# An LSTM with a three-layer network behind it: when VectorE does its side work in the first 21 steps

## The chip, the cores and the metric

The kernel runs on one core of a Trainium2 chip. The metric is the device time of one execution in microseconds (us), and of several runs the median. Engines are named as in the profile: PE is TensorE (PEld its weight loads), DVE is VectorE, ACT is ScalarE, POOL is GpSimd, SP is SyncE.

## The reference

x has shape (32, 64, 256): 32 rows, 64 time steps, 256 features. An LSTM with 256 hidden units runs over the 64 steps, starting from the hidden state `cond_1024` and a cell state of zero. A network of three layers, whose weights are signs (+1 or -1, given as booleans), runs on every hidden state, and its result is added to x.

```python
xW = einsum('ntd,dg->ntg', x, Wx) + b
a = xw_t + prev_h @ Wh                      # one step; scan over 64 steps
i, f, o = sigmoid(a[:, :H]), sigmoid(a[:, H:2*H]), sigmoid(a[:, 2*H:3*H])
g = tanh(a[:, 3*H:])
next_c = f * prev_c + i * g
next_h = o * tanh(next_c)
...
h = concatenate([hs, -hs], axis=-1)         # 512 wide
h = relu(s0 * (h @ sign(k0))) * 2           # 512 -> 1024
h = relu(s1 * (h @ sign(k1))) * 2           # 1024 -> 1024
out = x + s2 * (h @ sign(k2))               # 1024 -> 256
```

## The kernel before

The 32 rows and 4 quarters of the hidden units share the 128 partitions, so a gate tile is 128 by 4 gates by 64. The recurrence takes 64 steps, one turn of the loop over `t` each. The order in which every engine gets its instructions is written out by hand in that loop: an engine does them in the order of the program text.

**One step of the recurrence.** `gates_from_h` (L277) lets PE add the product of h with wh to the gate banks. `cell_step` follows: ACT takes sigmoid, tanh and sigmoid (L294 to L296), DVE computes `kept`, `new` and `c` (L298 to L302), ACT takes tanh of c (L304), DVE computes `h` (L306) and turns it by a transpose into `hist` (L311), from which the next step's matmuls read. Meanwhile ACT copies the next step's share of x into the gate banks (`gates_from_x`, L288 and L289). The time from one step's first L277 matmul to the next step's is called a step's period here.

**The work beside it.** After the cell, each step issues a share of other matmuls. In the first 21 steps (`X_STEPS`) these are the products of x with wx (`x_products`, L230), 208 parts in all; each two time steps of x fill one bank in 8 parts, and a step issues 10 parts (8 in step 10). From step 21 on they are the network on blocks of 16 steps (`ffn_block`): layer 0 at L429, layer 1 at L456, layer 2 at L443. The last block runs after the loop, and its end is `last_chunk`.

**What DVE does for it in the first 21 steps.** When a bank of x products is full, `evict_x` adds the bias while it moves the bank to SBUF (`xg`, L245; 128x512). `next_x` turns the next half block of x by a transpose (`turn_x`, L217, into `xT`; 128x512) and then has SP load a half block further on (`load_x`). Every fourth step `split_h` writes h of four steps as two parts: `hhi` on ACT (L326) and `hlo` on DVE (L327; 128x256). `make_w0` builds a quarter of the layer-0 weights, first on ACT (`w0t`, L193) and then on DVE (L194; 128x512).

**What ACT does for it.** Besides L193 and L326, `make_w1` writes one of eight rows of the layer-1 weights (L199, 128x1024) and then has SP load further bits; `make_w2` writes a quarter of the layer-2 weights (L203, 128x512).

The pieces of weights wait in one queue, `chores`: four of w0, eight of w1, four of w2. One is taken in each step from `FIRST_CHORE` = 4 on. In the text of a step, the ACT part of the chore comes before the x products, the DVE part of a w0 chore after them, and the split of h at the very end of the steps 3, 7, 11 and so on:

```python
        later = chores.popleft()() if t >= FIRST_CHORE and chores else None
        ...
        if callable(later):
            later()
        if t % SH == SH - 1:
            split_h(t // SH)
```

Of the kernel before, what the change touches and what calls it, by code (L numbers as in the profile page):

```python
# [38 lines left out]
def lstm_ffn(ctx: ExitStack, tc: tile.TileContext, x, cond, wx_d, wh_d, b_d, k0_d, k1_d, k2_d, s0_d, s1_d, s2_d, out):  # L39
# [10 lines left out]
    SB = 16  # L50
    NB = T // SB
    TB = SB * N
    SH = 4
# [3 lines left out]
    AHEAD = 12  # L57
    X_STEPS = 21

    FIRST_CHORE = 4  # L60
    WARM_UP = 8

    const = ctx.enter_context(tc.tile_pool(name="const", bufs=1))
# [11 lines left out]
    def act(shape, dtype, name):  # L75
        return apool.tile(shape, dtype, tag="act", name=name)
# [4 lines left out]
    def load_x(i, half, engines, part=slice(0, SB // 2)):  # L81
        if part.start == 0:
            xq[i, half] = xpool.tile([P, SB // 2, HQ], F32, tag="x", name=f"x{i}_{half}")
        t0 = i * SB + half * (SB // 2)
        for q in range(NQ):
            engines[q % len(engines)].dma_start(
                out=xq[i, half][q * N : (q + 1) * N, part],
                in_=x[:, t0 + part.start : t0 + part.stop, ts(q, HQ)],
            )
# [57 lines left out]
    for i in range(2):  # L147
        t = act([P, 2, F0], U8, f"k0_{i}")
# [49 lines left out]
    def make_w1(k):  # L198
        nc.scalar.activation(w1[:, k, :], bits[k], AF.Identity, bias=nsgn[1], scale=sgn2[1])  # L199
        load_bits(4 + k)  # L200

    def make_w2(k, m):
        nc.scalar.activation(  # L203
            w2[:, m, ts(k, 4)].rearrange("p k (q j) -> p k q j", q=NQ),
            bits[FC0 + k].rearrange("p (k q m j) -> p m k q j", k=4, q=NQ, m=2)[:, m],
            AF.Identity,
            bias=minus1,
            scale=2.0,
        )
# [4 lines left out]
    def turn_x(i, half, part=slice(0, SB // 2)):  # L214
        if part.start == 0:
            xT[i, half] = act([P, SB // 2, 2, N], F32, f"xT{i}_{half}")
        nc.vector.transpose(  # L217
            xT[i, half][:, part].rearrange("p t b n -> p (t b n)"),
            xq[i, half][:, part].rearrange("p t j -> p (t j)"),
        )  # L220
# [2 lines left out]
    wh_q = wh.rearrange("p k (g q j) -> p k q g j", g=4, q=NQ)  # L223
    xg = {}

    def x_part(p, t, k, slots, start):

        i, s = divmod(t, SB // 2)
        for q in range(NQ):
            nc.tensor.matmul(  # L230
                p[q * N : (q + 1) * N, t % 2, slots],
                xT[i // 2, i % 2][:, s, k, :],
                wx_q[:, k, q, slots],
                start=start,
                stop=False,
                skip_group_check=True,
            )

    def x_bank(t):
        return ps_f.tile([P, 2, 4, HQ], F32, tag="pf", name=f"px{t}")  # L240

    def evict_x(p, t):
        xg[t] = gpool.tile([P, 2, 4 * HQ], F32, tag="xg", name=f"xg{t}")
        b = bias[:, :4].rearrange("p g j -> p (g j)").unsqueeze(1).to_broadcast([P, 2, 4 * HQ])
        nc.vector.tensor_tensor(xg[t], p.rearrange("p t g j -> p t (g j)"), b, ALU.add)  # L245

    def next_x(half):

        if half < 2 * NB:
            turn_x(*divmod(half, 2))  # L250
            if half + 4 < 2 * NB:
                load_x(*divmod(half + 4, 2), [nc.sync])

    def x_products(t0, t1):

        for t in range(t0, t1, 2):
            p = x_bank(t)
            for s in range(2):
                for k in range(2):
                    x_part(p, t + s, k, slice(0, 4), s == 0 and k == 0)  # L260
                    if s == 1 and k == 1:
                        evict_x(p, t)
                        half, left = divmod(t + 2, SB // 2)
                        if left == SB // 4 and t + 2 != AHEAD:
                            next_x(half + 1)
                    yield 2


# [4 lines left out]
    def gates_from_h(t, hT):  # L273
        for g, slots in zip(gates, (slice(0, 3), slice(3, 4))):
            for k in range(2):
                for q in range(NQ):
                    nc.tensor.matmul(  # L277
                        g[q * N : (q + 1) * N],
                        hT[:, k, :],
                        wh_q[:, k, q, slots],  # L280
                        start=False,
                        stop=(k == 1),
                        skip_group_check=True,
                    )
# [6 lines left out]
    def cell_step(t, c):  # L291
        sig = cell.tile([P, 3, HQ], F32, tag="sig", name=f"sig{t}")
        cand = cell.tile([P, HQ], F32, tag="cand", name=f"cand{t}")
        nc.scalar.activation(sig[:, 0:2, :], gates[0][:, 1:3], AF.Sigmoid)  # L294
        nc.scalar.activation(cand, gates[0][:, 0], AF.Tanh)  # L295
        nc.scalar.activation(sig[:, 2, :], gates[1][:, 0], AF.Sigmoid)  # L296
        kept = cell.tile([P, HQ], F32, tag="kept", name=f"kept{t}")
        nc.vector.tensor_mul(kept, sig[:, 1, :], c)  # L298
        new = cell.tile([P, HQ], F32, tag="new", name=f"new{t}")
        nc.vector.tensor_mul(new, sig[:, 0, :], cand)  # L300
        c = cell.tile([P, HQ], F32, tag="c", name=f"c{t}")
        nc.vector.tensor_add(c, kept, new)  # L302
        th = cell.tile([P, HQ], F32, tag="th", name=f"th{t}")
        nc.scalar.activation(th, c, AF.Tanh)  # L304
        h = cell.tile([P, HQ], F32, tag="h", name=f"h{t}")
        nc.vector.tensor_mul(h, sig[:, 2, :], th)  # L306
        i, s = divmod(t, SH)
        if s == 0:
            hist[i] = hpool.tile([P, 2, SH * N], F32, tag="hist", name=f"hist{i}")
        hT = hist[i][:, :, ts(s, N)]  # L310
        nc.vector.transpose(hT, h.rearrange("p (b j) -> p b j", b=2))  # L311
        if t + 1 < T:
            gates_from_x(t + 1)
        return c, hT

    def split_h(i):

        b, s = divmod(i, SB // SH)
        if s == 0:
            hparts[b] = (  # L320
                hpool.tile([P, 2, TB], F32R, tag="hhi", name=f"hhi{b}"),
                hpool.tile([P, 2, TB], F32R, tag="hlo", name=f"hlo{b}"),
            )
        hi, lo = (p[:, :, ts(s, SH * N)] for p in hparts[b])
        full = hist.pop(i)
        nc.scalar.copy(hi, full)  # L326
        nc.vector.tensor_tensor(lo, full, hi, ALU.subtract)  # L327
# [171 lines left out]
    for k, t in [(k, t) for t0 in (0, SB // 4) for k in range(2) for t in range(t0, t0 + SB // 4)]:  # L499
        x_part(banks[t // 2], t, k, early, t % 2 == 0 and k == 0)  # L500
    for t in range(SB // 2):
        for k in range(2):
            x_part(banks[t // 2], t, k, late, False)
        if t % 2:
            evict_x(banks[t // 2], t - 1)
        if t == 1:
            turn_x(0, 1)
    nc.vector.transpose(hT, h_first.rearrange("p (b j) -> p b j", b=2))
    for _ in x_products(SB // 2, AHEAD):
        pass  # L510
# [3 lines left out]
    def ffn():  # L514
        for b in range(NB):
            yield from ffn_block(b)


    chores = deque()
    chores += [lambda k=k, h=h: make_w0(k, h) for k in range(2) for h in range(2)]  # L520
    chores += [lambda k=k: make_w1(k) for k in range(FC0)]
    chores += [lambda k=k, m=m: make_w2(k, m) for k in range(2) for m in range(2)]

    work = x_products(AHEAD, T)
    total_x = (T - AHEAD) * 4
    total_ffn = (NB - 1) * (4 * FC0 + 2 * FC0 * FC1 + 4 * FC1)
    done = 0
    for t in range(T):
        gates_from_h(t, hT)
        c, hT = cell_step(t, c)  # L530
        if t == 0:
            next_x(AHEAD // (SB // 2) + 1)
        later = chores.popleft()() if t >= FIRST_CHORE and chores else None
        if outputs and next(outputs[0], "end") == "end":
            outputs.popleft()
        if t == X_STEPS:
            work, done = ffn(), 0
        goal = (t + 1) * total_x // X_STEPS if t < X_STEPS else (t + 1 - X_STEPS) * total_ffn // (T - X_STEPS)
        while done < goal:
            done += next(work)  # L540
        if t == X_STEPS - 1:
            next(work, None)
        if callable(later):
            later()
        if t % SH == SH - 1:
            split_h(t // SH)
    for n, _ in enumerate(work):
        if outputs and n % 4 == 0 and next(outputs[0], "end") == "end":
            outputs.popleft()
# [28 lines left out]
```

## Time and profile before

| what | value |
|---|---|
| median of 3 runs | 318.73 us (318.44, 318.73, 320.07) |
| the profiled execution, own time | 318.87 us |
| its span | 317.1 us |
| PE, PEld, DVE, ACT, POOL busy | 307.1, 237.5, 154.4, 130.1, 7.6 us |
| mean granted TensorE clock | 0.997 |
| first gates matmul of step 0 | at 19.84 us of the span |
| first gates matmul of step 21 | at 84.25 us of the span |

The median is the time to be predicted. The profiled execution is a run of its own: its time is the span that the trace covers and 1.77 us around it. "Busy" is time in which an engine had at least one instruction of its own in work. Matmuls overlap, so the busy time of PE says that it had work, not that it ran at its peak. In the timeline, a row gives the start, the length, the engine, the source line, the operation, what it writes and reads, and after an x the number of instructions that the row holds.

### The profile page before, as it was taken

The page shows a single profiled execution, that of the slowest core. Times are in us where ns is not written, and L with a number is a line of the kernel's source. Part 1 is how long each engine was busy: PE and PEld are TensorE (multiplying, and loading weights), DVE is VectorE, ACT ScalarE, POOL GpSimd, SP SyncE. Part 2 cuts the span into 40 slices and gives each one's busy share as a digit, 9 for nine tenths or more (in the row PEclk, how much of TensorE's full clock was granted, in tenths as well). Part 3 has the DMA queues.
Part 4 walks back from the last instruction along what each step waited for, and adds up shares of the span by engine and source line. Part 5 has one row for each costly group of instructions (what it writes and reads, how often), then busy time and mean ns, then how long its engine had stood idle before and what let it go on. Part 6 is the DMA issues. An engine that isn't in the chain of part 4 may idle for free.

```text
span 317.1 us, 9519 instructions
## 1 busy us (share of the span) xinstructions
PE 307.1 (97%) x4026; PEld 237.5 (75%) x4026; DVE 154.4 (49%) x475; ACT 130.1 (41%) x483; POOL 7.6 (2%) x26
## 2 busy tenths in 40 slices
PE   6789999999999999999999999999999999999994
PEld 3767777777877777777777777777777777888893
DVE  1355886756674443334845433466543433911124
ACT  0214557775563433334633434355333432511110
POOL 4400000000000000000000000000000000000000
PEclk9999999999999999999999999999999999999998
DMA  5755301142000000000010100000310000230002
GB/s 133 187 137 157 83 2 37 52 102 56 5 0 2 2 0 2 1 2 2 2 34 13 24 1 2 2 0 20 83 34 3 2 0 2 55 77 2 0 0 66
DMA packets 31001, 10.99 MB, mean 35 GB/s; under 512 B 28072, under 2 KB 30376, under 8 KB 30960
## 3 DMA queue, kind: packets, MB, share of 16 engines
q1 hardware_dynamic: 27648, 8.66, 11.4%
q10 hardware_dynamic: 3040, 1.57, 2.0%
q8 instruction: 31, 0.51, 0.7%
q0 software_dynamic: 272, 0.17, 0.2%
q14 instruction: 10, 0.08, 0.1%
HBM read 8.29 MB, written 2.10 MB: 33 GB/s over the span
## 4 chain that ended last, share of the span: by engine, by line
PE 89%; DMA 6%; DVE 3%; ACT 1%; issue 0%; ACTq 0%; SPq 0%; DVEq 0%
PE p L456 37%; PE gates L277 19%; PE px L230 12%; PE p L429 10%; PE po L443 7%; DMA x<-in_x_dram 2%; PE po L395 2%; DMA wx<-in_L_cond_Wx_dram 2%; PE p L383 1%; DMA wh<-in_L_cond_Wh_dram 1%; DVE xg L245 1%; DVE w L194 0%; ACT th L304 0%; DVE h L306 0%; DVE c L302 0%
## 5 line engine op out<-in xcount | busy, mean ns | idle before, releaser
L277 PEld LDWEIGHTS gates<-wh,hist 128*32 128x32 f32 x2016 | 54.3, 109 | 25.4 <-issue 14.1
L277 PE MATMUL gates<-wh,hist 128*32 128x192 f32 x2016 | 68.1, 275 | 0.4 <-DVE hist L311 0.3
L230 PE MATMUL px<-wx,xT 128*32 128x256 f32 (+1 forms) x1152 | 60.6, 356 | 2.8 <-DMA wx<-in_L_cond_Wx_dram 1.2
L294 ACT ACTIVATE sig<-gates 128x128 f32<-128x128 f32 x64 | 17.8, 278 | 81.5 <-PE gates L277 81.1
L230 PEld LDWEIGHTS px<-wx,xT 128*32 128x32 f32 x1152 | 39.8, 110 | 14.8 <-issue 2.2
L298 DVE TENSOR_TENSOR kept<-sig,c 128x64 f32<-128x64 f32 x63 | 14.1, 224 | 59.5 <-ACT sig L294 59.2
L304 ACT ACTIVATE th<-c 128x64 f32<-128x64 f32 x64 | 16.5, 257 | 31.2 <-DVE c L302 31.2
L429 PE MATMUL p<-hhi,w 128*128 128x512 f32 x64 | 25.5, 398 | 0.0
L429 PE MATMUL p<-hlo,w 128*128 128x512 f32 x64 | 25.3, 395 | 0.0
L306 DVE TENSOR_TENSOR h<-sig,th 128x64 f32<-128x64 f32 x64 | 14.5, 226 | 20.7 <-ACT th L304 20.7
L245 DVE TENSOR_TENSOR xg<-px,bias 128x512 f32<-128x512 f32 x32 | 20.9, 663 | 5.9 <-POOL nsgn L162 4.2
L288 ACT COPY gates<-xg 128x192 f32<-128x192 f32 x64 | 20.1, 313 | 0.0
L311 DVE STREAM_TRANSPOSE hist<-h 128x64 f32<-128x64 f32 x64 | 15.7, 246 | 2.4
L302 DVE TENSOR_TENSOR c<-kept,new 128x64 f32<-128x64 f32 x64 | 14.4, 225 | 2.2
L296 ACT ACTIVATE sig<-gates 128x64 f32<-128x64 f32 x64 | 15.0, 234 | 0.0
L429 PEld LDWEIGHTS p<-hhi,w 128*128 128x128 f32 x64 | 12.0, 188 | 2.8
L295 ACT ACTIVATE cand<-gates 128x64 f32<-128x64 f32 x64 | 14.0, 219 | 0.0
L300 DVE TENSOR_TENSOR new<-sig,cand 128x64 f32<-128x64 f32 x64 | 13.9, 218 | 0.0
L429 PEld LDWEIGHTS p<-hlo,w 128*128 128x128 f32 x64 | 12.0, 188 | 2.6
L289 ACT COPY gates<-xg 128x64 f32<-128x64 f32 x64 | 13.1, 204 | 0.0
L456 PE MATMUL p<-a_7h,w 128*128 128x512 f32 x31 | 12.6, 407 | 0.0
L456 PE MATMUL p<-a_2l,w 128*128 128x512 f32 x31 | 12.5, 404 | 0.0
(181 smaller groups left out, 516.7 us busy)
## 6 DMA issues: line engine op xcount, KB each, us to landing
x<-in_x_dram SPq DMA_DIRECT2D x58, 64.0 KB, 2.4
out_dram<-o SPq DMA_DIRECT2D x28, 64.0 KB, 1.8
bits<-in_L_ffn_k_dram SPq DMA_DIRECT2D x10, 128.0 KB, 2.8
wx<-in_L_cond_Wx_dram SPq DMA_DIRECT2D x8, 64.0 KB, 3.2
wx<-in_L_cond_Wx_dram ACTq DMA_DIRECT2D x8, 64.0 KB, 3.2
k<-in_L_ffn_k_dram SPq DMA_DIRECT2D x8, 64.0 KB, 2.6
wh<-in_L_cond_Wh_dram SPq DMA_DIRECT2D x2, 192.0 KB, 4.5
wh<-in_L_cond_Wh_dram ACTq DMA_DIRECT2D x2, 192.0 KB, 5.2
```

The lines of the kernel that those rows point to most:

```text
L230: nc.tensor.matmul(p[q * N : (q + 1) * N, t % 2, slots], xT[i // 2, i % 2][:, s, k, :], wx_q[:, k, q, slots], start=start, stop=False, ski ...
L245: nc.vector.tensor_tensor(xg[t], p.rearrange("p t g j -> p t (g j)"), b, ALU.add)
L277: nc.tensor.matmul(g[q * N : (q + 1) * N], hT[:, k, :], wh_q[:, k, q, slots], start=False, stop=(k == 1), skip_group_check=True,)
L288: nc.scalar.copy(gates[0], x_t[:, :3])
L294: nc.scalar.activation(sig[:, 0:2, :], gates[0][:, 1:3], AF.Sigmoid)
L296: nc.scalar.activation(sig[:, 2, :], gates[1][:, 0], AF.Sigmoid)
L304: nc.scalar.activation(th, c, AF.Tanh)
L306: nc.vector.tensor_mul(h, sig[:, 2, :], th)
L311: nc.vector.transpose(hT, h.rearrange("p (b j) -> p b j", b=2))
L429: nc.tensor.matmul(p, w0[:, k, ts(m, P)], a[:, k, :], start=(n == 0), stop=(n == 3))
L443: nc.tensor.matmul(po[m], w2[:, m, k], a1[k][n], start=(k == 0 and n == 0), stop=(k == FC1 - 1 and n == 1))
L456: nc.tensor.matmul(p1[m], w1[:, k, ts(m, P)], a0[k][n], start=(k == 0 and n == 0), stop=(k == FC0 - 1 and n == 1),)
```

## The change

The loop gets a count, `load`, of the bias additions and turns of x that a step has put on DVE. Turns of x are no longer done where they fall due: `x_products` puts them into a queue, `turns`, earlier than before (after the second time step of a half block instead of the fourth), and one is taken at the end of a step that has fewer than two such operations. If one is still waiting after the sixth time step, it is done there. The turn that step 0 did right after the cell now goes this way too, behind the step's bias addition.

The split of h goes into a queue, `splits`. It is taken at the end of a step with a count below two, and at the latest four steps after it fell due; from step 21 on it is taken at once, as before. A step that takes a split takes no chore. The chores start in step 2 instead of 4. The DVE part of a w0 chore goes into a queue as well, `w0_parts`, and is taken at the end of a step with a count below two, or in step 20. The four w2 chores have a queue of their own and start in step 24.

The resulting order, with the DVE work behind the cell in each of the first steps:

| step | before | after |
|---|---|---|
| 0 | turn, addition | addition, turn |
| 1 | addition | addition |
| 2 | addition | addition, turn |
| 3 | addition, turn, addition, split | two additions |
| 4 | addition, w0 | addition, split |
| 5 | addition, w0 | addition, turn |
| 6 | addition, turn, w0 | addition, w0 |
| 7 | two additions, w0, split | two additions |
| 8 | addition | addition, turn |
| 9 | addition, turn | addition, split |
| 10 | addition | addition, w0 |
| 11 | addition, split | addition, split |
| 12 | two additions, turn | two additions |
| 13 | addition | addition, turn |
| 14 | addition | addition, w0 |
| 15 | addition, split | addition, turn |
| 16 | addition, turn, addition | two additions |
| 17 | addition | addition, split |
| 18 | addition | addition, w0 |
| 19 | addition, split | addition, split |
| 20 | two additions | two additions |

On ACT, the w0 pieces move from steps 4 to 7 to steps 2, 3, 5 and 6; the w1 pieces from steps 8 to 15 to steps 7, 8, 10 and 12 to 16; the w2 pieces from steps 16 to 19 to steps 24, 25, 26 and 28. The order of PE's matmuls and of SP's loads is the same in both kernels, and so is the number of instructions on each engine.

```diff
-    FIRST_CHORE = 4
+    FIRST_CHORE = 2
+    W2_STEP = 24
...
+    load = [0]
+    turns = deque()
+
...
     def evict_x(p, t):
...
+        load[0] += 1
         nc.vector.tensor_tensor(xg[t], p.rearrange("p t g j -> p t (g j)"), b, ALU.add)
 
     def next_x(half):
 
         if half < 2 * NB:
+            load[0] += 1
             turn_x(*divmod(half, 2))
...
                         half, left = divmod(t + 2, SB // 2)
-                        if left == SB // 4 and t + 2 != AHEAD:
-                            next_x(half + 1)
+                        if left == 2 and half + 1 < 2 * NB:
+                            turns.append(half + 1)
+                        if left == 6 and turns:
+                            next_x(turns.popleft())
...
-    chores += [lambda k=k, m=m: make_w2(k, m) for k in range(2) for m in range(2)]
+    chores2 = deque(lambda k=k, m=m: make_w2(k, m) for k in range(2) for m in range(2))
+    splits, w0_parts = deque(), deque()
...
     for t in range(T):
+        load[0] = 0
         gates_from_h(t, hT)
         c, hT = cell_step(t, c)
-        if t == 0:
-            next_x(AHEAD // (SB // 2) + 1)
-        later = chores.popleft()() if t >= FIRST_CHORE and chores else None
+        if t % SH == SH - 1:
+            splits.append(t // SH)
...
-        if callable(later):
-            later()
-        if t % SH == SH - 1:
-            split_h(t // SH)
+
+        if turns and load[0] < 2:
+            next_x(turns.popleft())
+        if splits and (load[0] < 2 or t >= X_STEPS or t == SH * splits[0] + 2 * SH - 1):
+            split_h(splits.popleft())
+        else:
+            if t >= FIRST_CHORE and chores:
+                part = chores.popleft()()
+                if part is not None:
+                    w0_parts.append(part)
+            elif t >= W2_STEP and chores2:
+                chores2.popleft()()
+            if w0_parts and (load[0] < 2 or t == X_STEPS - 1):
+                w0_parts.popleft()()
```

## The prediction, written before the changed kernel ran

> **What bounds the kernel now.** I read the page's busy line first. PE is busy for 97% of the span, DVE for 49%:
>
> ```profile
> PE 307.1 (97%) x4026; PEld 237.5 (75%) x4026; DVE 154.4 (49%) x475; ACT 130.1 (41%) x483; POOL 7.6 (2%) x26
> ```
>
> So a change to DVE's work can pay only where DVE makes PE late. The table of stages shows where to look: from 100 to 260 us PE is busy in every microsecond, so the network steps have no hole that this change could fill. The holes lie before 20 us, where loads are awaited and which the change leaves alone, and in the stage of the x products, 20 to 85 us. There I went through PE's timeline, whose rows alternate between the gates matmuls (L277) and a step's x products (L230). These are steps 3, 4 and 5, then 8 to 11, then 18 and 19:
>
> ```profile
> 28.93 1.08 PE L277 MATMUL gates<-wh,hist 128*32 128x192 f32 x32
> 31.96 1.08 PE L277 MATMUL gates<-wh,hist 128*32 128x192 f32 x32
> 35.26 1.08 PE L277 MATMUL gates<-wh,hist 128*32 128x192 f32 x32
> ...
> 44.35 1.08 PE L277 MATMUL gates<-wh,hist 128*32 128x192 f32 x32
> 47.87 1.08 PE L277 MATMUL gates<-wh,hist 128*32 128x192 f32 x32 [0.27 <-DVE hist L311]
> 50.90 1.08 PE L277 MATMUL gates<-wh,hist 128*32 128x192 f32 x32
> 51.77 1.94 PE L230 MATMUL px<-wx,xT 128*32 128x256 f32 x32
> 53.78 1.08 PE L277 MATMUL gates<-wh,hist 128*32 128x192 f32 x32
> ...
> 75.03 1.08 PE L277 MATMUL gates<-wh,hist 128*32 128x192 f32 x32
> 78.19 1.08 PE L277 MATMUL gates<-wh,hist 128*32 128x192 f32 x32
> ```
>
> The usual period is 3.03 us (28.93 to 31.96): 72 matmuls that PE issues without a gap. Step 10 has 32 x products instead of 40 and a period of 2.88 us (50.90 to 53.78); there PE waits, and 2.88 us is what the chain gates, sigmoid, cell, `hist`, gates itself takes. The chain thus has 3.03 - 2.88 = 0.15 us to spare in a usual step. Steps 4 and 8 take 3.30 and 3.52 us, 0.27 and 0.49 too long. Step 13 takes 3.06, step 17 3.04, step 18 3.16. From step 0 to step 21 the trace has 84.25 - 19.84 = 64.41 us; twenty periods of 3.03 and one of 2.88 make 63.48. All that can be won in this stage is 0.93 us.
>
> The full timeline shows why step 4 is long:
>
> ```profile
> 31.59 0.65 DVE L245 TENSOR_TENSOR xg<-px,bias 128x512 f32<-128x512 f32 x1
> 32.16 0.69 DVE L217 STREAM_TRANSPOSE xT<-x 128x512 f32<-128x512 f32 x1
> 32.78 0.65 DVE L245 TENSOR_TENSOR xg<-px,bias 128x512 f32<-128x512 f32 x1
> 32.94 0.28 ACT L294 ACTIVATE sig<-gates 128x128 f32<-128x128 f32 x1 [0.84 <-PE gates L277]
> 33.35 0.40 DVE L327 TENSOR_TENSOR hlo<-hist,hhi 128x256 fp32r<-128x256 f32 x1
> 33.68 0.21 DVE L298 TENSOR_TENSOR kept<-sig,c 128x64 f32<-128x64 f32 x1
> ```
>
> An undisturbed `kept` starts 0.31 us after its `sig` (29.91 to 30.22), so here 33.25 would have been in time. It started at 33.68, 0.43 late, because step 3 had queued four operations ahead of it. With 0.15 to spare that makes 0.28, and PE shows 0.27. Step 8 checks this: `sig` at 45.33, `kept` at 46.29, 0.65 late, less 0.15 is 0.50; PE shows 0.49. In steps 7, 13 and 17 `kept` is 0.16, 0.21 and 0.18 late (42.77, 61.34 and 73.46, against `sig` at 42.30, 60.82 and 72.97), which costs 0.00, 0.03 and 0.01. So the rule that I use is: period = 3.03 + (lateness of `kept` - 0.15), where that is positive.
>
> **The change part by part.** *Fewer operations behind the cell.* The tails of steps 3, 7, 12 and 16 (which made steps 4, 8, 13 and 17 late) become two additions each. DVE's room runs from the end of `hist` (28.64) to the next `kept` (30.22), 1.58 us. Two additions took 1.25 us in step 7 (44.13), 1.33 in step 20 (83.87), where the second starts after its bank is full. They fit, so the four long periods fall to 3.03: 0.27 + 0.49 + 0.03 + 0.01 = 0.80 us saved.
>
> *What is late next.* The fullest new tails are addition and turn (steps 0, 2, 5, 8, 13, 15) and addition and w0 part (6, 10, 14, 18). Both exist before: addition and turn in step 9 ended at 51.79 with `kept` at 52.19; addition and w0 part in step 4 ended at 36.43 with `kept` at 36.55, on time. In steps 0, 8 and 13 the bank is full only with the fourth of five parts; such an addition (step 17, 74.86) took 0.69 instead of 0.65 and was done 0.67 after `hist`, so with 0.69 of turn the tail ends 1.36 after it, inside 1.58. Step 0 may start 0.15 later, since its turn no longer fills the wait for the bank; that still ends at about 1.51. I charge nothing; the cover is 0.07 to 0.3 us of room and 0.15 of spare chain, and beyond it each further 0.1 us costs 0.1 in each of six steps. PE then finds nothing else late: 3.03 us is its own issue.
>
> *Turned x for PE.* A turn is needed when the next half block's first x product issues. The tightest is step 13 (before: step 12): its products come after the third part of step 14, about 1.1 us after the turn ends. The others lie whole steps ahead. Cost nothing. The four loads that SP issues behind each turn move with it, by at most 3 us of a queue that then has nothing else due; the bits behind the w1 pieces are loaded a step earlier for the first and at most one later for the last.
>
> *Chores on ACT.* ACT's room is the same stretch. A w0 piece (0.72 us) in steps 2 and 3 meets room of 1.45 us (the idle time before `sig` at 29.91). A w1 piece of 1.24 us fits: in step 9 it ended at 51.61 with `sig` at 51.88. Before, steps 11 and 15 held a w1 piece and the split, 1.24 + 0.39; after, a split has its step for itself. The first w0 piece now stands at about 28.45 at the head of ACT's queue, and everything of ACT waits behind it if k0 has not landed; SP issued k0's last load at 24.2 and the slowest took 3.3, so it is there by 27.5. Cost nothing; the next use is far: the last w0 part in step 18 against layer 0 at 85.26, the last w1 piece in step 16 against layer 1 at 95.1.
>
> *w2 in the network steps.* Four pieces of 0.72 us join ACT in steps 24, 25, 26 and 28. Steps there take 4.18 or 4.41 us against a chain of 2.88. The worst is step 26: the eviction `a_2h` starts at 109.89 and ends at 110.49, the piece runs to about 111.21, and `sig`, which came at 110.77, waits 0.44 us. `hist` then ends at 113.02 instead of 112.58, still 0.94 before the gates matmuls at 113.96. Layer 2 first reads w2 at 110.79, the pieces of steps 24 and 25 by then done. Cost nothing; without that cover, 0.44 for this piece and at most 4 x 0.72 = 2.88 for all.
>
> *Unknown.* Step 18's extra 0.13 has another face: `sig` started 1.25 us after the gates matmuls instead of 0.98, with ACT idle. No row says why. Since instructions move, it may vanish (-0.13) or strike elsewhere; bounded by its 0.27 of lateness, it is -0.13 to +0.27 and I take zero.
>
> The sum: 318.87 - 0.80 = 318.07 for the profiled execution. The median stands 0.14 below that execution, so 318.73 - 0.80 = 317.93, a change of -0.25%. About 0.5%, 1.6 us, is what a measurement of this kernel can tell from no change.
>
> **Rivals.** *Nothing moves.* The view of waits puts only 0.3 us of PE's idle time on `hist`, in one step, and four of the six addition-and-turn tails come where there was less before. If the new tails each give back a little, the gain is 0 to 0.3 us: 318.4 to 318.7. Against it: the rule above reproduces all five late periods within 0.02 us. The Trainium skill ("Perfetto Trace Analysis", Identifying the Most-Contended Engine) says to find the engine with the highest occupancy and optimize that first; by it, work on DVE at 49% beside PE at 97% would leave 318.73. The trace disagrees in part: in two steps of 64 DVE's queue does set PE's start.
>
> *The w2 pieces hold up the network steps (slower).* If ACT's queue in steps 24 to 28 decided PE's start, each piece would cost up to its 0.72: 318.73 - 0.80 + 2.88 = 320.8. It decides once the lateness of `sig` passes 0.94 us in step 26, against my 0.44; two pieces in one step would be needed. For it speaks only that these are the one place where the change adds work.
>
> *A smaller loss of the same kind:* 0 to 1.6 us lost to new waits (late k0, late banks, a stray late `sig`), 318.7 to 320.3.
>
> *More than 0.93 us gained* would need a second mechanism, of which the trace shows none.
>
> **How the numbers follow.** Forecast, -0.65 to -0.93 us: 0.68. Nothing moves: 0.15. The small loss: 0.08. The w2 pieces, or another loss above 1.6 us: 0.06. A gain above 1.6 us: 0.03. Within 0.5% lie the first three, 0.91. The range begins at 318.73 - 0.93 - 0.29 = 317.5 (everything won, and the 0.29 by which the fastest run shown lies below the median) and ends at 318.73 + 0.44 = 319.1 (nothing won, and step 26's piece uncovered). It holds the first two cases and a third of the small loss.
>
> **What would show it.** Right: periods of 3.03 in steps 4 and 8, no `kept` more than 0.15 behind its time in steps 0 to 20, step 21 starting at about 83.45 instead of 84.25, and from there to the end the same length as before. Wrong: a period above 3.05 in steps 1, 3, 6, 9, 14 or 16 (behind addition and turn); an ACT idle time before the first w0 piece put on k0; PE idle between 97 and 115 us; or the stage shortened and the time unchanged.

## The result and the profile after

The changed kernel takes 317.63 us in the median of 22 runs, the kernel before 318.40 in 22. The ratio is 0.9967, with a 95% interval of 0.9955 to 0.9979: 0.33% faster, and this interval leaves no room for "no change". (0.9967 is also the ratio of the means; the medians differ by 0.77 us, 0.24%.) The forecast was 317.93. The profiled execution took 318.01 us with a span of 316.2 (before 318.87 and 317.1).

From the page of the changed kernel come the busy line and the line with the engines' shares of the chain that ended last:

```profile
PE 306.8 (97%) x4026; PEld 238.4 (75%) x4026; DVE 155.5 (49%) x475; ACT 130.2 (41%) x483; POOL 7.6 (2%) x26
PE 91%; DMA 6%; DVE 1%; ACT 0%; issue 0%; SPq 0%; ACTq 0%
```

The busy shares are those of before to the percent. What changed is the second line. In the profile of before it reads:

```profile
PE 89%; DMA 6%; DVE 3%; ACT 1%; issue 0%; ACTq 0%; SPq 0%; DVEq 0%
```

DVE's share fell from 3% to 1%, and PE's rose from 89% to 91%. DVE works as much as it did, but no longer in the way.

PE's timeline after, the gates matmuls of steps 3 to 5, 8 to 10, and 18 and 19:

```profile
28.98 1.08 PE L285 MATMUL gates<-wh,hist 128*32 128x192 f32 x32
32.01 1.08 PE L285 MATMUL gates<-wh,hist 128*32 128x192 f32 x32
35.04 1.08 PE L285 MATMUL gates<-wh,hist 128*32 128x192 f32 x32
...
44.14 1.08 PE L285 MATMUL gates<-wh,hist 128*32 128x192 f32 x32
47.17 1.08 PE L285 MATMUL gates<-wh,hist 128*32 128x192 f32 x32
50.20 1.08 PE L285 MATMUL gates<-wh,hist 128*32 128x192 f32 x32
...
74.30 1.08 PE L285 MATMUL gates<-wh,hist 128*32 128x192 f32 x32
77.33 1.08 PE L285 MATMUL gates<-wh,hist 128*32 128x192 f32 x32
```

Steps 4 and 8 now take 3.03 us each (32.01 to 35.04, 44.14 to 47.17), where they took 3.30 and 3.52; step 18 takes 3.03 instead of 3.16; and the remark that PE waits for `hist` is gone. From the full timeline of the tail behind step 7, which held four operations before, these are DVE's rows and the first sigmoid:

```profile
43.59 0.24 DVE L319 STREAM_TRANSPOSE hist<-h 128x64 f32<-128x64 f32 x1
43.76 1.33 DVE L250 TENSOR_TENSOR xg<-px,bias 128x512 f32<-128x512 f32 x2
45.11 0.28 ACT L302 ACTIVATE sig<-gates 128x128 f32<-128x128 f32 x1 [0.28 <-PE gates L285]
45.42 0.23 DVE L306 TENSOR_TENSOR kept<-sig,c 128x64 f32<-128x64 f32 x1 [0.33 <-ACT sig L302]
```

The two additions end at 45.09, before `sig` has even started, and `kept` follows 0.31 us behind `sig`, on time.

To compare kernels I take the time from the first sigmoid of step 0 to that of step 21 (the stage of the x products), and from there to that of step 63. Beside them stand the start of the first sigmoid and the timed result as a ratio to before with its interval:

| kernel | step 0 starts, us | step 0 to 21 | 21 to 63 | ratio |
|---|---|---|---|---|
| before | 20.82 | 64.40 | 179.20 | 1 |
| changed | 20.86 | 63.51 | 179.21 | 0.9967 (0.9955 to 0.9979) |
| `again` | 20.25 | 63.51 | 179.20 | 0.9986 (0.9969 to 1.0003) |
| `turns_only` | 21.61 | 64.06 | 179.21 | 1.0008 (0.9989 to 1.0026) |
| `parts_only` | 21.15 | 63.53 | 179.20 | 0.9978 (0.9958 to 0.9999) |
| `w2_late` | 20.76 | 64.27 | 179.22 | 0.9996 (0.9976 to 1.0016) |
| `extra1` | 21.43 | 64.76 | 179.20 | 0.9999 (0.9980 to 1.0018) |
| `extra2` | 20.96 | 78.49 | 179.20 | 1.0430 (1.0404 to 1.0455) |
| `one_more` | 20.99 | 64.28 | 179.20 | 0.9976 (0.9959 to 0.9993) |
| `two_more` | 21.66 | 63.67 | 179.20 | 0.9977 (0.9963 to 0.9990) |

The stage is 64.40 - 63.51 = 0.89 us shorter, and nothing behind it moved. The start of step 0 scatters over 1.4 us between these executions, more than the effect, so the timed ratios, of 4 to 12 runs each below the row of the changed kernel, can't tell the middle rows apart; the stage can, to a few hundredths. The 0.89 us is 0.28% of the time, inside the interval of the timed ratio. An interval that excludes 1 is not enough by itself: that of `one_more` does so too, though its stage is only 0.12 us, or 0.04% of the time, shorter. What ties the gain to the change is the stage, not the timed ratio alone.

### The profile page after: what moved, and what is told of

Its sections match the earlier page's. It is cut to its first block, busy times and chain, and to the rows that moved or that the text cites. A ratio compares the mean times of both kernels' runs of the same rounds, so it can differ in the third digit from the quotient of the medians.

```text
span 316.2 us, 9515 instructions
## 1 busy us (share of the span) xinstructions
PE 306.8 (97%) x4026; PEld 238.4 (75%) x4026; DVE 155.5 (49%) x475; ACT 130.2 (41%) x483; POOL 7.6 (2%) x26
## 4 chain that ended last, share of the span: by engine, by line
PE 91%; DMA 6%; DVE 1%; ACT 0%; issue 0%; SPq 0%; ACTq 0%
PE p L464 37%; PE gates L285 20%; PE px L234 14%; PE p L437 10%; PE po L451 7%; DMA x<-in_x_dram 3%; PE po L403 2%; DMA wx<-in_L_cond_Wx_dram 2%; PE p L391 1%; DMA wh<-in_L_cond_Wh_dram 1%; DVE a_7l L345 0%; SPq L87 0%; DVE o L370 0%; DVE o L367 0%; ACT sig L302 0%
## 5 line engine op out<-in xcount | busy, mean ns | idle before, releaser
L285 PEld LDWEIGHTS gates<-wh,hist 128*32 128x32 f32 x2016 | 55.1, 109 | 23.6 <-issue 13.4
```

What stands on the lines that cost most here:

```text
L285: nc.tensor.matmul(g[q * N : (q + 1) * N], hT[:, k, :], wh_q[:, k, q, slots], start=False, stop=(k == 1), skip_group_check=True,)
```

## The experiments

**The changed kernel again.**

> The changed kernel once more. Theory (VectorE's queue behind the cell made four gate starts late, and nothing else changed): every period from step 0 to step 20 is 3.03 us (2.87 in step 10), the first gates matmul of step 21 comes 63.5 us after that of step 0 (64.4 before), and the time is about 0.8 us below before. Rival (the medians of the two kernels differ by more than that because of how the execution starts or ends): the difference between executions of this kernel lies ahead of the first gates matmul (19.89 us in its first trace) or behind the last one, at the same 63.5 us between.

The stage is 63.51 us again. The span fell from 316.2 to 315.6, and all of it lies ahead of step 0, whose matmuls started 0.62 us earlier; the shorter wait of PE for a load of x is 0.40 of it. PE's timeline of `again`:

```profile
19.27 1.08 PE L285 MATMUL gates<-wh,hT_first 128*32 128x192 f32 x32 [0.59 <-DMA x<-in_x_dram]
```

In the changed kernel's first trace this row stood at 19.89 with a wait of 0.99. So the theory holds for the stage, and the rival for the difference between these two executions, which lies ahead of step 0. The 0.89 us is not part of that. The time itself was a miss: about 0.8 us below before was expected, and these 12 runs have a median 0.45 us below (318.49 against 318.94), with an interval of 0.9969 to 1.0003 that does not exclude "no change".

**One part of the change at a time.** `turns_only` is the kernel before with this change alone (the count of operations goes with it):

```diff
-                        if left == SB // 4 and t + 2 != AHEAD:
-                            next_x(half + 1)
+                        if left == 2 and half + 1 < 2 * NB:
+                            turns.append(half + 1)
+                        if left == 6 and turns:
+                            next_x(turns.popleft())
...
-        if t == 0:
-            next_x(AHEAD // (SB // 2) + 1)
...
+        if turns and load[0] < 2:
+            next_x(turns.popleft())
         if callable(later):
             later()
```

> The kernel before with the turns of x queued as in the change, and the splits and weight pieces as they were. Theory, with the rule period = 3.03 + (lateness of kept - 0.15) and the tails of this order (two additions, w0 part and split in step 7 are left): kept is about 0.54 late in step 8 and 0.17 in step 6, so 64.3 - 0.4 = 63.9 us from step 0 to step 21, half of the gain. Rival (the turns make the gain, by way of loads and turned x that come earlier): 63.5.

`parts_only` is the changed kernel with the first lines put back:

```diff
-                        if left == 2 and half + 1 < 2 * NB:
-                            turns.append(half + 1)
-                        if left == 6 and turns:
-                            next_x(turns.popleft())
+                        if left == SB // 4 and t + 2 != AHEAD:
+                            next_x(half + 1)
...
         c, hT = cell_step(t, c)
+        if t == 0:
+            next_x(AHEAD // (SB // 2) + 1)
```

> The changed kernel with the turns of x where they were; splits, w0 parts and w2 pieces wait as in the change. Theory: steps 3, 12 and 16 still hold two additions and a turn, which makes kept 0.12 to 0.18 late in steps 4, 13 and 17, so nearly inside the 0.15 to spare: 63.5 to 63.6 us from step 0 to step 21, almost the whole gain. Rival (the turns make the gain): 64.3.

`turns_only` has 64.06 us: step 4 is cured, step 8 is not. From its timeline behind step 7, DVE's rows and the first sigmoid:

```profile
44.50 1.33 DVE L249 TENSOR_TENSOR xg<-px,bias 128x512 f32<-128x512 f32 x2
45.75 0.74 DVE L194 SCALAR_TENSOR_TENSOR w<-k,nsgn,w0t 128x512 fp32r<-128x512 uint8 x1
45.85 0.28 ACT L301 ACTIVATE sig<-gates 128x128 f32<-128x128 f32 x1 [0.50 <-PE gates L284]
46.41 0.42 DVE L334 TENSOR_TENSOR hlo<-hist,hhi 128x256 fp32r<-128x256 f32 x1
46.74 0.22 DVE L305 TENSOR_TENSOR kept<-sig,c 128x64 f32<-128x64 f32 x1
```

`kept` should have come at 45.85 + 0.31 = 46.16 and came at 46.74, 0.58 late (0.54 expected); the rule charges 0.58 - 0.15 = 0.43, and the period is 3.46. Most of what lies above the expected 63.9 is a late sigmoid in step 18 (0.12), treated below. `parts_only` has 63.53: behind step 3 it still queues addition, turn and addition.

```profile
33.27 0.28 ACT L300 ACTIVATE sig<-gates 128x128 f32<-128x128 f32 x1 [0.80 <-PE gates L283]
33.69 0.20 DVE L304 TENSOR_TENSOR kept<-sig,c 128x64 f32<-128x64 f32 x1
```

`kept` is 0.42 behind `sig`, 0.11 late, and the period stays 3.03, as the 0.15 to spare says; only step 13, 0.22 late, shows 3.06. The two parts overlap, since either one cures step 4. Letting the splits and w0 parts wait was nearly the whole cure, and on top of it the earlier turns added 0.02.

**More work in the tails.** `extra1` and `extra2` add one and two more operations to VectorE's tail:

```diff
+    spare = const.tile([P, 2, 4 * HQ], F32, name="spare")
+
+    def extra(t):
+        b = bias[:, :4].rearrange("p g j -> p (g j)").unsqueeze(1).to_broadcast([P, 2, 4 * HQ])
+        nc.vector.tensor_tensor(spare, xg[t // 2 * 2], b, ALU.add)
...
+        if t < X_STEPS - 1:
+            for _ in range(1):        # 2 in extra2
+                extra(t)
```

> The changed kernel with one more bias addition of 128x512 (into a tile that nobody reads) at the end of VectorE's tail in each of the steps 0 to 19. Theory, by the rule with the tails of this order: kept comes 0.1 to 0.35 us late in most steps, of which 0.15 is spare, so 64.7 us from step 0 to step 21 instead of 63.5, 1.2 us lost for 12 us of added work. Rival (VectorE at 49% is not what bounds the stage): 63.5, no loss.

> The same with two more additions in each of the steps 0 to 19. Theory: now every step is the length of chain and tail together, kept is 0.6 to 0.9 late in nearly all, and the stage takes 75.7 us: the second 12 us of work cost 11. Rival (a busy share matters, not the place): 63.5 to 64.7 and no kink between one and two additions.

64.76 us was measured against 64.7 expected: 20 added operations, some 12 us of VectorE's work, cost 1.25. The second 20 operations cost 13.7, since now nearly every step is as long as its chain and tail. 78.49 is 2.8 above the expected 75.7. DVE's rows in one tail of `extra2` point to what was mis-sized:

```profile
45.12 0.65 DVE L250 TENSOR_TENSOR xg<-px,bias 128x512 f32<-128x512 f32 x1
45.70 0.73 DVE L195 SCALAR_TENSOR_TENSOR w<-k,nsgn,w0t 128x512 fp32r<-128x512 uint8 x1
46.35 1.41 DVE L256 TENSOR_TENSOR spare<-xg,bias 128x512 f32<-128x512 f32 x2
47.67 0.22 DVE L312 TENSOR_TENSOR kept<-sig,c 128x64 f32<-128x64 f32 x1
```

The two added ones occupy 47.67 - 46.35 = 1.32, or 0.66 each. The expectation does not give what it put for one; 2.8 us over 40 operations is 0.07, which brings it to about 0.59, near the 0.60 from start to start of two additions from a bank (1.25 - 0.65). That this was the mis-sized term is worked back, not shown. The rule itself holds in these long steps: the `sig` of this step starts at 46.32, so `kept` is 47.67 - 46.32 - 0.31 = 1.04 late, the rule gives 3.03 + 0.89 = 3.92, and the period is 3.91. The kink between one and two is there, and busy share is not what prices VectorE's work here.

**The w2 pieces alone.** The kernel before with the four w2 pieces in the steps where the change has them:

```diff
-    chores += [lambda k=k, m=m: make_w2(k, m) for k in range(2) for m in range(2)]
+    chores2 = [lambda k=k, m=m: make_w2(k, m) for k in range(2) for m in range(2)]
+    chores2 = dict(zip((24, 25, 26, 28), chores2))
...
+        if t in chores2:
+            chores2[t]()
```

> The kernel before with only the four w2 pieces moved from steps 16 to 19 to steps 24, 25, 26 and 28. Theory: VectorE's order is that of before, so 64.3 us from step 0 to step 21 (64.4 if step 18's late sigmoid comes again) and the time of before within 0.1 us. Rival (taking work off ScalarE in the x steps makes part of the gain): less than 64.2, periods 4 and 8 shorter than 3.30 and 3.52. Second rival (the pieces cost time in the network steps): a gap of PE between steps 25 and 29 and up to 2.9 us more.

Periods 4 and 8 are 3.29 and 3.51, so taking work off ScalarE cures neither. The network steps take 179.22 us: the pieces cost nothing there. But the stage is 64.27, 0.13 shorter than before. All of it is in step 18, whose sigmoid is on time.

**The late sigmoid of step 18.** ScalarE's timeline of before and of the changed kernel:

```profile
76.28 0.28 ACT L294 ACTIVATE sig<-gates 128x128 f32<-128x128 f32 x1 [0.92 <-PE gates L277]
76.46 0.22 ACT L295 ACTIVATE cand<-gates 128x64 f32<-128x64 f32 x1
76.56 0.23 ACT L296 ACTIVATE sig<-gates 128x64 f32<-128x64 f32 x1
```

```profile
75.27 0.28 ACT L302 ACTIVATE sig<-gates 128x128 f32<-128x128 f32 x1 [1.12 <-PE gates L285]
75.45 0.22 ACT L303 ACTIVATE cand<-gates 128x64 f32<-128x64 f32 x1
75.78 0.22 ACT L304 ACTIVATE sig<-gates 128x64 f32<-128x64 f32 x1
```

Before, the first of the three starts 1.25 us after the gates matmuls (75.03) instead of 0.98. After, the first two are on time and the third comes 0.51 us behind the first instead of 0.28. The delay has not gone, it has moved by two instructions, to where `h` does not need the result yet. Counted along ScalarE's instruction list, the late one is number 149 in both: the changed kernel has two instructions fewer ahead of step 18. Two kernels test this by the number alone:

```diff
     nc.scalar.activation(warm[:, 1:2], warm[:, :1], AF.Sigmoid)
+    nc.scalar.activation(warm[:, 2:3], warm[:, :1], AF.Sigmoid)      # one_more: before with this line
+    nc.scalar.activation(warm[:, 3:4], warm[:, :1], AF.Sigmoid)      # two_more: changed kernel with both
```

> The kernel before with one more instruction at the head of ScalarE's list (the tiny warm-up sigmoid a second time). Theory (the sigmoid that came 0.27 us late in step 18 did so because of its place in ScalarE's instruction list: in six traces it is always the instruction that stands at number 149 which starts 0.23 to 0.27 us late): the first sigmoid of step 18 is now number 150 and on time, number 149 is the w2 piece of step 17, period 17 of the sigmoids is 3.04 instead of 3.31, and 64.27 us from step 0 to step 21 instead of 64.40. Rival (it has to do with the w2 pieces, which stood beside it in both kernels that showed it): period 17 stays at 3.31.

> The changed kernel with two more of the tiny warm-up sigmoids at the head of ScalarE's list, so that number 149 of the list, which was the third activation of step 18, is its first one. Theory (the number decides): the first sigmoid of step 18 comes 0.27 us late again, period 17 of the sigmoids is 3.30 instead of 3.03, and the stage takes 63.63 us instead of 63.51, though VectorE's order is the changed one. Rival (the changed order itself removed it): 63.5 and no period above 3.05.

`one_more` did as expected: the sigmoid of step 18 is on time, period 17 is 3.03, the stage 64.28. An instruction more made the stage 0.12 us shorter. `two_more` was half a miss. The stage grew to 63.67, about as much as expected, but by luck, since it grew in another place: period 3 is 3.35, because the first sigmoid of step 4 is late. The rows of steps 3 and 4, then the first two of step 18:

```profile
30.75 0.28 ACT L304 ACTIVATE sig<-gates 128x128 f32<-128x128 f32 x1 [0.80 <-PE gates L287]
34.10 0.28 ACT L304 ACTIVATE sig<-gates 128x128 f32<-128x128 f32 x1 [1.11 <-PE gates L287]
...
76.23 0.28 ACT L304 ACTIVATE sig<-gates 128x128 f32<-128x128 f32 x1 [1.12 <-PE gates L287]
76.54 0.22 ACT L305 ACTIVATE cand<-gates 128x64 f32<-128x64 f32 x1
```

The late sigmoid of step 4 is number 51 in this list. In the changed kernel number 51 is the third activation of step 4, and there it was 0.14 late, unseen (it started at 33.41, the first of the three at 32.99, usually 0.28 ahead). In step 18 of `two_more` the first sigmoid was on time and `cand`, number 150, was 0.13 late. So the place in the list decides and the order of VectorE does not, but by this count "number 149" is exact only to an instruction. Number 349 is late too (step 45, in before and the changed kernel alike, where a network step has room).

The count becomes exact once it takes in ScalarE's semaphore instructions, which the trace holds and the timeline leaves out. Number 192 is then the late instruction of step 18 in all kernels but `one_more`, and in `two_more` `cand` is that number. Number 64 is the first sigmoid of step 4 in `two_more`, and in the changed kernel a semaphore instruction just ahead of the third activation; number 448 is the late one of step 45, in the kernels that have one there. These places lie 128 or 256 apart. In `one_more` number 192 is a semaphore instruction that waits for PE in any case, and nothing near it is late; there number 576, the third activation of step 58, starts 0.24 late, again 128 further on. What happens at these places, no run here settles.

**A version with fewer x steps.** PE's own pace is all that is left in the stage, except for step 10, where PE waits 0.28 us in a period of 2.87. `x20` spreads the x products over 20 steps:

```diff
-    X_STEPS = 21
+    X_STEPS = 20
```

> The changed kernel with the x products in 20 steps instead of 21 (the network starts in step 20). The step with four pieces and a period of 2.87 us, in which PE waits 0.28 us for the chain, is gone; some steps get six pieces and take about 3.46. Theory (PE is the only bound left in this stage): from the first sigmoid to the 64th 242.4 us instead of 242.7, and 0.3 us less in all. Rival (steps of six pieces with two additions, a turn or a w0 part are late again): periods above 3.03 in steps of five pieces, or above 3.46 in steps of six, and the 0.3 us not seen.

From the first sigmoid to the 64th it takes 242.78 us against 242.72: no gain, though every period is 3.03 or 3.46 as the theory wants. (Its timed ratio is 0.9963, 0.9947 to 0.9979, the same as the changed kernel's.) The 0.28 was given back in a place that the expectation left out. A step of the recurrence that moves from the x products to the network pays more for its gates matmuls. From PE's timeline of the changed kernel, with eleven network matmuls left out at the mark:

```profile
95.86 0.39 PE L464 MATMUL p<-a_3l,w 128*128 128x512 f32 x1
96.18 1.08 PE L285 MATMUL gates<-wh,hist 128*32 128x192 f32 x32
97.19 0.50 PE L464 MATMUL p<-a_4h,w 128*128 128x512 f32 x1
97.53 0.40 PE L464 MATMUL p<-a_4l,w 128*128 128x512 f32 x1
...
100.36 1.08 PE L285 MATMUL gates<-wh,hist 128*32 128x192 f32 x32
```

Between 96.18 and 100.36 lie 13 network matmuls, 0.2275 us apart (97.99 to 99.81 holds eight), 2.96 us, which leaves 1.22 for the gates. In an x step the products are issued in pieces of eight matmuls, five to a step, or six in some steps of `x20`; a piece costs 0.43 (3.46 - 3.03), five cost 2.15, and 0.88 is left for the gates. 1.22 - 0.88 = 0.34 lost, 0.28 gained: 0.06 longer, as measured. By these marks none of the versions run beats the changed kernel.

## Why the prediction was right or wrong

*The bound and the rule.* Right. The late periods became 3.03, and the rule also gave the lateness of step 8 in `turns_only` (0.54 against 0.58), the absorbed 0.11 of `parts_only`, the stage of `extra1` within 0.06 us, and the period of a step of `extra2` within 0.01.

*The sum.* 0.80 us was forecast and 0.89 came in the stage: 0.77 from steps 4, 8, 13 and 17 (0.27, 0.48, 0.02, and 0.00 as read from the sigmoids) and 0.12 from step 18. The term of the sum that was mis-sized is the one headed "unknown": I took zero between -0.13 and +0.27, and it was -0.12, because the two instructions fewer on ScalarE moved the delay out of the way. That was luck: the place in the list could have gone the other way, as `two_more` shows (+0.16). The forecast of 317.93 lies 0.30 above the median of 317.63 for a reason outside the change: it starts from the median of three runs, 318.73, and 22 runs of the same kernel have 318.40. That the two medians of 22 differ by 0.77, so near to the 0.80, is partly luck as well, with starts that scatter by more than that.

*What is late next.* Right: all six addition-and-turn tails kept `kept` within 0.01 us of its time, step 0 included. Turned x, k0 and the weight pieces delayed nothing.

*w2 in the network steps.* The mechanism was right and its size not: in step 26 the piece ran from 109.55 and `sig` came at 110.16, 0.23 late instead of the 0.44 forecast, because the piece starts before the eviction ahead of it has ended and `sig` before the piece has. Nothing came of it: 179.21 us against 179.20.

*What failed* is the step behind the sum, the judgement on what a measurement can tell from no change. I called about 0.5%, 1.6 us, the limit, gave no working for it, and put 0.91 on a change inside it, so that my own 0.80 us counted as no change. With 22 runs of each kernel the interval is 0.12% to either side, about 0.4 us, a quarter of the limit that I put; the change of 0.33% is clear of it, and it is faster and not "no change". The trace would have shown the change at any such limit: the stage repeats to 0.01 us in the two executions of the changed kernel, and differs by 0.89 from before. The range, 317.5 to 319.1, holds the median of 317.63 near its lower end.

*The rivals.* "Nothing moves" is out: the stage is 0.89 us shorter in two traces of two. The rule that the Trainium skill gives ("Perfetto Trace Analysis", Identifying the Most-Contended Engine), to optimize the engine with the highest occupancy first, judges PE by the share of its peak that it reaches and by the busy share of its weight loads, not by that of its matmuls. The profile gives the second, 75% before, and by it the rule names PE here as well. That a change to VectorE's order then gains nothing was the prediction's own step from it, and the runs refute that step: 0.77 us came from VectorE's order while its busy share stayed at 49%. PE did set the pace of nearly all steps, and the whole gain is 0.3%.

## What to carry to other kernels

Beside a recurrence, the price of side work is set by the room in its own step. Work out the chain's slack (here a step with less PE work showed it, 3.03 - 2.88), add up each step's queue ahead of the chain's next operation, and charge only what exceeds room plus slack; the same operation costs nothing in one step and its whole length in another. When an effect is smaller than the scatter of the start, compare two fixed marks inside the trace.

## What the runs showed of the hardware

ScalarE starts some instructions 0.13 to 0.31 us late by their place in its instruction list (numbers 64, 192, 448 and 576, semaphore instructions counted), so one tiny instruction more made one kernel's stage 0.12 us shorter, and two made another's 0.16 longer.

32 gates matmuls take 0.88 us of PE between x products of the same 32-row form and 1.22 us between 128-row network matmuls, counted from the spacing of the matmuls around them.
